# The mask as the start value of each dot, and a divided unit's first part added by TensorE (graph attention on one Trainium2 core)

## The chip, the core and the metric

The kernel runs on one core of a Trainium2 chip. Five engines run at the same time, each with its own in-order queue: TensorE (PE, with a separate row PEld for its weight loads), VectorE (DVE), ScalarE (ACT), GpSimd (POOL) and SyncE (SP, which here only issues transfers). They wait for each other by semaphores. The metric is the device time of one execution, in microseconds (us). Before the change the median of 12 runs is 2206.37 us (2199.12 to 2210.2).

## What is computed

Two graph attention layers over 2048 nodes with 256 channels and 8 batches. A node attends only to its neighbours in `adj`, each layer adds its input and normalises. The change touches layer 0 only:

```python
h1 = x @ W1; h2 = x @ W2; h3 = x @ W3
e = einsum('bnd,bmd->bnm', h1, h2)
e = leaky_relu(e, 0.2)
e = where(adj > 0, e, -1e12)
h_prime = softmax(e) @ h3
x = layernorm(x + relu(h_prime))
```

Layer 1 has four heads and additive scores (a term of the row plus a term of the neighbour), then softmax, weighted sum, elu and a layer norm.

## The kernel before

A node has on average about 17 neighbours, so nothing dense is computed. In the set-up, nodes are counted and sorted by their number of neighbours and cut into 16 tiles of 128 nodes, one node to a partition. Tile t gets `SLOTS[t]` neighbour slots (36 down to 11); slot k of a tile is a gather of 128 rows, the k-th neighbour of each node. Where a node has fewer neighbours than its tile has slots, `neg` (128 partitions by 291 columns, one column to a slot, made at L553) holds -3.0e38 instead of 0, and the slot's index points nowhere, so that the row keeps what stood there.

The work unit is a tile and one half of the batches (4 of 8). Layer 0 runs 16 units of the first half (h = 0), then 16 of the second; layer 1 runs its 32 units behind them. Within a layer 0 unit:

- `own_rows` and `before0` fetch the tile's own rows, turn them (PE, evicted by ACT) and project them with W1 W2^T to `u.g` (PE L437, evicted by ACT at L642).
- GpSimd issues one gather per slot (L200) into a ring of buffers; a buffer comes free when PE has used it in the sum.
- `logits0` takes the slots in order. `dots` (L648) forms, for each slot and each of 4 batches, the product of the gathered row and `u.g` summed over 256 channels: one DVE instruction (L651), followed by a read of its accumulator into one column of the score tile `e`. When all slots of a part are there, leaky relu (L692), mask (L693), maximum (L702) and subtraction (L703) follow on DVE, and ACT makes the exponential.
- `weights0` sums and divides. `weighted` makes of each weight a diagonal of 64 columns on ACT (L861, four per slot).
- `sums0` multiplies diagonals and gathered rows on PE and adds them up in two PSUM accumulators per part (`add_slot`, L825).
- `after0`: `whole` brings the sum to `u.hs`, `turn_h` turns it on PE, `project_h` multiplies with W3 (PE L437), `residual` adds the input and takes statistics (DVE L979, L982), then the norm (ACT L415) and the query projection for layer 1 (PE L1020).

A unit with `SLOTS` of 16 or more (11 of the 16 tiles; t = 0 too, which has 26 main slots and one slot for all of its further neighbours) is divided: `parts` has two entries, each with its own softmax so that the first part's sum can start early. When the second part's maximum and sum are known, the first part's share is known too. At the fifth slot of the second part ACT writes the first part's accumulators, scaled by that share, to `u.hs` (L948):

```python
if i == 1 and k == 4:
    u.hs = hs_rows
    ...
        u.hs[:, ts(2 * r + j, C)], u.accs[0][r][:, ts(j, C)], AF.Copy,
```

and after the last slot DVE adds the second part's accumulators (L962, two additions of 128x512). For a unit that is not divided ACT copies the accumulators (L966).

The order on DVE, ACT and PE is written by the kernel itself: `tick` advances a clock by one per slot of `sums0`, and in each tick it takes what is due. `due(distance, stage)` puts a stage that many ticks ahead: `whole` 4 ticks after a divided unit's last slot, `turn_h` 2 ticks later, `project_h` 4 more. The dots of later units are interleaved in this order. In each queue an instruction that waits holds up all behind it. The tile t = 0 has a path of its own for its further neighbours: `extra_logits0` forms their dots at L651 as well (8 of them, against `u.gx` in PSUM), and `into_place` (L748) copies the spread result into `e`.

The 2248 dots against `u.g` are 281 main slots by 4 batches by 2 halves.

Of the kernel before, what the change touches and what calls it, by code (L numbers as in the profile page):

```python
# [19 lines left out]
ALU = mybir.AluOpType  # L20
# [4 lines left out]
P = 128  # L25
# [15 lines left out]
EXTRA = SLOTS[0] - MAIN  # L41
# [95 lines left out]
def fast_path(  # L137
# [24 lines left out]
    nc = tc.nc  # L162
    B, N, C = x.shape
    NT = N // P
    KC = C // P
    HB = B // 2
    HC = HB * C
    MOST = 2 + MAIN // 2 + EXTRA
    HG = HB * H
    HW = HC // 2  # L170
    CD = C + H
    QW = 2 * CD
    offs = [sum(SLOTS[:t]) for t in range(NT)]
# [53 lines left out]
    held = [ring_tile(f"held_{i}") for i in range(MORE)]  # L227
# [3 lines left out]
    ident = w.ident  # L231

    g_rows = held[0][:, : 2 * HC].rearrange("p (i c) -> p i c", i=2)
    xo_rows, hs_rows = held[1][:, :HC], held[1][:, HC : 2 * HC]

    twice = const.tile([P, 64], F32, tag="twice", name="twice")
    nc.vector.tensor_tensor(twice, ident[:, :64], ident[:, 64:], ALU.add)
# [3 lines left out]
    for it in range(NT):  # L241
        r = ring_tile(f"adj_{it}")
# [56 lines left out]
    for it in range(NT):  # L299
# [6 lines left out]
        i = it // 2  # L306
# [31 lines left out]
    neg = const.tile([P, total], F32, tag="neg", name="neg")  # L338
# [4 lines left out]
    for r in range(2):  # L343
        rr = slice(64 * r, 64 * r + 64)
        pr = ps_tile(f"ps_half_{r}")[:, :NT]
        for c in range(2):
            nc.tensor.matmul(
                pr[64 * c : 64 * c + 64],
                lhsT=ident[rr, rr],
                rhs=ranked[rr, 0, :],  # L350
                start=True,
                stop=True,
                tile_position=(64 * r, 64 * c),
# [66 lines left out]
    def due(distance, stage, *args):  # L420
        heappush(events, (clock[0] + distance, len(stamps), partial(stage, *args)))
        stamps.append(None)
# [222 lines left out]
            yield  # L645
        u.ready = True

    def dots(u, rows, others, into):  # L648
        for b in range(HB):
            jt = sp.tile([P, C], BF16, tag="j", name=f"j_{u.name}_{clock[0]}_{b}", bufs=4)  # L650
            nc.vector.tensor_tensor_reduce(  # L651
                out=jt,
                in0=rows[:, ts(b, C)],
                in1=others(b),
                scale=1.0,
                scalar=0.0,
                op0=ALU.mult,
                op1=ALU.add,
                accum_out=into(b),
            )  # L660

    def logits0(u):

        while not u.ready:
            yield 0
        for i, part in enumerate(u.parts):
            n, o = f"{u.name}_{i}", offs[u.t] + part.at
            K = part.wide
            if i == 0:
                both = ep.tile([P, 2, HB, MOST], F32, tag="e", name=f"e_{n}")  # L670
            e = both[:, i, :, : 1 + K + 1]
            if part.extra:
                yield from extra_logits0(u, i, e)
            for k in range(part.main):
                if i == 0 and k == part.main - 4 and u.parts[-1].extra:
                    due(0, spread_g, u)
                c, s = part.where(k)
                while len(u.chunks[i]) <= c:
                    yield 0
                while clock[0] < u.chunks[i][c][2] + 3:  # L680
                    yield 0
                dots(
                    u,
                    u.chunks[i][c][0][:, s, :],
                    lambda b: u.g[:, ts(b, C)],
                    lambda b, k=k: e[:, b, 1 + k : 2 + k],
                )
                yield 1
            while part.extra and not u.placed:
                yield 0  # L690
            p = e[:, :, 1 : 1 + K]
            nc.vector.scalar_tensor_tensor(p, p, ALPHA, p, ALU.mult, ALU.max)  # L692
            nc.vector.tensor_tensor(  # L693
                p, p, neg[:, o : o + K].unsqueeze(1).to_broadcast([P, HB, K]), ALU.add
            )
            v = p
            if i:
                v = e[:, :, : 1 + K]
                nc.vector.tensor_copy(e[:, :, 0], u.m[0])
            m = sp.tile([P, HG], F32, tag="m1", name=f"m_{n}")[:, :HB]  # L700
            u.m.append(m)
            nc.vector.tensor_reduce(m, v, AX.X, ALU.max)  # L702
            nc.vector.tensor_tensor(  # L703
                v, v, m.unsqueeze(2).to_broadcast([P, HB, v.shape[2]]), ALU.subtract
            )
            due(2, nc.scalar.activation, v, v, AF.Exp)
            due(4, weights0, u, i, K, e, m)
            yield 0
# [9 lines left out]
    def extra_logits0(u, i, e):  # L718
        main = u.parts[i].main
        while not u.chunks[i] or u.gx is None:  # L720
            yield 0
        while clock[0] < u.chunks[i][0][2] + 3:
            yield 0
        b = wide_tile(f"xe_{u.name}")
        x, ex = b[:, :HB], b[:, 16 : 16 + HB * EXTRA]
        ex = ex.rearrange("p (b k) -> p b k", b=HB)
        dots(
            u,
            u.chunks[i][0][0][:, 0, :],
            lambda b: u.gx[b // 2][:, ts(b % 2, C)],  # L730
            lambda b: x[:, b : b + 1],
        )
        nc.vector.tensor_tensor(
            ex,
            x.unsqueeze(2).to_broadcast([P, HB, EXTRA]),
            place.unsqueeze(1).to_broadcast([P, HB, EXTRA]),
            ALU.mult,
        )

        def to_rows():  # L740
            pe = ps_tile(f"ps_xe_{u.name}")[:, : HB * EXTRA]
            nc.tensor.matmul(
                pe, lhsT=of_one, rhs=b[:, 16 : 16 + HB * EXTRA], start=True, stop=True
            )
            due(2, into_place, pe)

        def into_place(pe):
            nc.vector.tensor_copy(  # L748
                e[:, :, 1 + main : 1 + main + EXTRA], pe.rearrange("p (b k) -> p b k", b=HB)
            )  # L750
            u.placed = True

        due(1, to_rows)
        yield 1
# [76 lines left out]
                        tile_position=(64 * r, 64 * c),  # L831
                    )

    def add_extra(acc, rows, lhsT, width):
        for r in range(2):
            for j in range(2 * C // width):
                for c in range(2):
                    rhs = rows[:, ts(2 * c + j, C)]
                    if width > C:
                        rhs = rows[:, ts(c, 2 * CD)].rearrange("p (j w) -> p j w", j=2)[:, :, :C]  # L840
                    nc.tensor.matmul(
                        acc[r][64 * c : 64 * c + 64, ts(j, width)],
                        lhsT=lhsT(r, c, j),
                        rhs=rhs,
                        start=False,
                        stop=(j == 2 * C // width - 1),
                        tile_position=(0, 64 * c),
                    )

# [74 lines left out]
    def sums0(u):  # L924
        u.accs = []
        for i, part in enumerate(u.parts):
            acc = None
            for k in range(part.K):
                while len(u.diags) <= part.at + k:
                    yield 0  # L930
                if acc is None:
                    acc = [acc_tile(f"acc_{u.name}_{i}_{r}") for r in range(2)]
                diag = u.diags[part.at + k]
                c, s = part.where(k) if k < part.main else (0, 0)
                rows, n, _ = u.chunks[i][c]
                if k < part.main:
                    add_slot(acc, k, part.K, rows[:, s, :], diag)
                else:
                    add_extra(
                        acc, rows[:, 0, :], lambda r, c, j: diag[r][:, 2 * c + j, :], C  # L940
                    )
                if s == n - 1:
                    credits[0] += 1
                if i == 1 and k == 4:
                    u.hs = hs_rows
                    for r in range(2):
                        for j in range(2):
                            nc.scalar.activation(  # L948
                                u.hs[:, ts(2 * r + j, C)], u.accs[0][r][:, ts(j, C)], AF.Copy,
                                scale=u.fs[:, r, j : j + 1],  # L950
                            )
                yield 1
            u.accs.append(acc)

    def after0(u):
        h, t, n = u.h, u.t, u.name

        def whole():
            if len(u.parts) == 2:
                for r in range(2):  # L960
                    v = u.hs[:, ts(r, HW)]
                    nc.vector.tensor_tensor(v, v, u.accs[1][r], ALU.add)  # L962
            else:
                u.hs = hs_rows
                for r in range(2):
                    nc.scalar.copy(u.hs[:, ts(r, HW)], u.accs[0][r])  # L966
# [86 lines left out]

        split = len(u.parts) == 2
        at = 4 if split else 2
        due(at, whole)
        due(at + 2, turn_h)
        due(at + 6, project_h)
# [320 lines left out]
    for j, u in enumerate(units):  # L1379
# [9 lines left out]
        if 2 <= j < 10:  # L1389
            b, i = divmod(j - 2, 2)  # L1390
# [317 lines left out]
```

## Time and profile before

| | us |
|---|---|
| median of 12 runs | 2206.37 |
| the profiled execution, its own time | 2207.72 |
| its span, first to last instruction | 2206.0 |
| set-up, 0 to 118: DVE busy | 73.08 |
| layer 0, 118 to 1255: DVE / PE / ACT / POOL busy | 1051.49 / 1018.50 / 817.71 / 715.56 of 1137 |
| layer 1, 1255 to 2206: DVE / PE / ACT / POOL busy | 832.49 / 658.16 / 526.61 / 702.16 of 951 |
| dots L651: busy, and their accumulator reads | 798.0 and 180.0 |
| mask additions L693, 54 of them: busy | 11.1 |
| additions L962, 44 of them: busy | 28.1 |
| diagonals L861, 2248 of them on ACT: busy | 570.3 |

The granted TensorE clock is 0.912 of full speed over the span. "Busy" is the time covered by an engine's records; records of consecutive DVE instructions overlap by some tens of nanoseconds, since the next starts before the last has drained, so sums of record lengths come out above the time that they hold the engine. A group line gives line, engine, operation, what it writes from what, shapes, count, then busy us, mean ns of one, and the idle time of the engine just before with what ended it.

### The profile page before, as it was taken

The numbers are of one execution on the slowest core, as the hardware profiler recorded it, in microseconds if no ns is written. First come the engines' busy times: TensorE is split into PE (matmuls) and PEld (weight loads), VectorE is DVE, ScalarE is ACT, GpSimd is POOL, SyncE is SP. The second block draws the span as 40 slices with busy tenths as digits, with TensorE's granted clock in tenths as the row PEclk, the third lists the DMA queues.
The fourth block names the chain that finished last, engine by engine and source line by source line (L and its number), as shares of the span: only waits on it lengthen the run. The fifth ranks groups of instructions, "written<-read, shape, count | busy, mean of one in ns | idle before, by whom it ended". The sixth has DMA issues, their size and how long they took to land. (4 is left out here: it accounts for less than half of the span.)

```text
span 2206.0 us, 50366 instructions
## 1 busy us (share of the span) xinstructions
PE 1696.7 (77%) x16096; PEld 917.2 (42%) x16096; DVE 1957.1 (89%) x6803; ACT 1399.1 (63%) x4801; POOL 1459.9 (66%) x1423
## 2 busy tenths in 40 slices
PE   0328798989889999999999887766666667776764
PEld 0215566656656666767666532221221212222221
DVE  7578889999999987799999779997987988998996
ACT  6306587768667776888888676543565656554545
POOL 3355476666666665667667577777777777777773
PEclk9659999999999999999999999898888898888887
DMA  9987899999998898999999899999999999999991
GB/s 389 316 276 247 307 336 386 351 333 332 330 320 291 305 326 272 347 347 361 341 350 343 289 380 367 344 345 353 388 359 346 363 371 363 379 348 356 367 339 58
DMA packets 240192, 734.76 MB, mean 333 GB/s; under 512 B 53984, under 2 KB 63328, under 8 KB 237488
## 3 DMA queue, kind: packets, MB, share of 16 engines
q0 software_dynamic: 183296, 645.85, 79.9%
q1 hardware_dynamic: 55360, 84.44, 11.5%
q8 instruction: 131, 2.15, 0.4%
q10 hardware_dynamic: 1264, 1.18, 0.2%
q14 instruction: 141, 1.16, 0.1%
HBM read 674.53 MB, written 76.09 MB: 340 GB/s over the span
## 5 line engine op out<-in xcount | busy, mean ns | idle before, releaser
L200 POOL DMA_INDIRECT s<-xg,idx x564 | 597.2, 1059 | 369.4 <-PE acc L825 134.2
L651 DVE CUSTOM_DVE_ANT_0 j<-s,held 128x256 bf16<-128x256 f32 x2248 | 798.0, 419 | 44.3 <-DMA s<-xg,idx 33.4
L825 PE MATMUL acc<-s,ident 64*64 64x512 f32 x4496 | 610.8, 685 | 262.8 <-DVE s L908 160.1
L200 POOL DMA_INDIRECT s<-qg,idx x564 | 574.4, 1018 | 181.4 <-issue 123.1
L825 PE MATMUL acc<-s,dg 64*64 64x256 f32 x8992 | 598.1, 394 | 69.1 <-ACT dg L861 68.6
L861 ACT ACTIVATE dg<-twice,e 128x64 f32<-128x64 f32 x2248 | 570.3, 341 | 36.8 <-PE acc L825 18.7
L908 DVE TENSOR_TENSOR s<-s,p 128x2048 f32<-128x2048 f32 (+1 forms) x246 | 542.4, 2208 | 0.1
L825 PEld LDWEIGHTS acc<-s,ident 64*64 64x64 f32 x4496 | 182.2, 151 | 679.7 <-issue 353.0
L825 PEld LDWEIGHTS acc<-s,dg 64*64 64x64 f32 x8992 | 342.0, 136 | 282.6 <-ACT dg L861 137.2
L898 ACT ACTIVATE s<-s,e 128x64 f32<-128x64 f32 x1376 | 342.5, 335 | 69.8 <-DVE e L1163 56.3
L1359 ACT ACTIVATE e<-e 128x40 f32<-128x40 f32 (+19 forms) x88 | 27.6, 313 | 285.1 <-DVE e L1143 185.3
L651 DVE DVE_READ_ACCUMULATOR2_ANT e<- 128x1 f32 x2248 | 180.0, 80 | 0.0
L208 POOL DMA_INDIRECT out_dram<-o,oidx x128 | 126.8, 991 | 64.2 <-ACT o L415 28.6
L1020 PE MATMUL ps_q<-wqs,x1T 128*128 128x264 f32 x512 | 136.7, 411 | 18.2 <-DVE y L979 11.3
L437 PE MATMUL ps_p_g<-held,xT 128*128 128x256 f32 x512 | 122.6, 394 | 0.0
L437 PE MATMUL ps_p_h<-held,hT 128*128 128x256 f32 x512 | 119.5, 386 | 0.0
L1087 DVE TENSOR_TENSOR e<-s,own 128x32 f32<-128x32 f32 (+1 forms) x290 | 52.8, 185 | 75.0 <-DMA s<-qg,idx 74.5
L1020 PEld LDWEIGHTS ps_q<-wqs,x1T 128*128 128x128 f32 x512 | 95.2, 196 | 57.4 <-issue 15.9
L1359 ACT COPY held<-ps_q 128x264 f32<-128x264 f32 x128 | 47.3, 379 | 104.1 <-PE ps_q L1020 93.3
L437 PEld LDWEIGHTS ps_p_g<-held,xT 128*128 128x128 f32 x512 | 97.5, 195 | 23.5 <-issue 8.1
L437 PEld LDWEIGHTS ps_p_h<-held,hT 128*128 128x128 f32 x512 | 95.0, 190 | 24.8 <-issue 12.4
L397 ACT ACTIVATE z<-st,roots 128x4 f32<-128x4 f32 x64 | 19.0, 297 | 126.8 <-DVE st L1266 99.1
(190 smaller groups left out, 1550.5 us busy)
## 6 DMA issues: line engine op xcount, KB each, us to landing
adj<-in_adj_dram SPq DMA_DIRECT2D x16, 1024.0 KB
xr<-held SPq DMA_DIRECT2D x128, 128.0 KB
x1s<-y SPq DMA_DIRECT2D x32, 512.0 KB
xr<-x1s SPq DMA_DIRECT2D x32, 512.0 KB
s<-xg,idx POOLq DMA_INDIRECT x564
s<-qg,idx POOLq DMA_INDIRECT x564
edges<-adj SPq DMA_DIRECT2D x16, 512.0 KB
xg<-in_x_dram SPq DMA_DIRECT2D x4, 2048.0 KB
```

Source lines behind the costliest of these rows:

```text
L200: nc.gpsimd.indirect_dma_start(out=dst, out_offset=None, in_=table, in_offset=AT(ap=index, axis=0), bounds_check=table.shape[0] - 1, oob_i ...
L208: ins = nc.gpsimd.indirect_dma_start(out=table, out_offset=AT(ap=index, axis=0), in_=src, in_offset=None)
L397: nc.scalar.activation(z, var, AF.Ln, bias=w.roots[:, 0:1], scale=1.0 / C)
L437: nc.tensor.matmul(pp[:, ts(j, C)], lhsT=srcT[:, ts((2 * i + j) * KC + k, P)], rhs=weight[:, k, :], start=(k == 0), stop=(k == KC - 1),)
L651: nc.vector.tensor_tensor_reduce(out=jt, in0=rows[:, ts(b, C)], in1=others(b), scale=1.0, scalar=0.0, op0=ALU.mult, op1=ALU.add, accum_out ...
L825: nc.tensor.matmul(out, lhsT=lhsT, rhs=rhs, start=(k == 0 and j == 0), stop=(k == K - 1 and (j == 1 or diag is None)), tile_position=(64 * ...
L861: nc.scalar.activation(diag[:, b, :], twice, AF.Copy, scale=u.p[i][:, b, k : k + 1])
L898: nc.scalar.activation(v[:, a, g, :], v[:, a, g, :], AF.Copy, scale=pv[:, a, g : g + 1])
L908: nc.vector.tensor_tensor(v, v, pv.unsqueeze(3).to_broadcast([P, n, H, D]), ALU.mult)
L1020: nc.tensor.matmul(pq[:, : C + 2 * H], lhsT=u.x1T[:, ts(i * KC + k, P)], rhs=w.sqs[:, k, j * H : j * H + CD + H], start=(k == 0), stop=(k ...
L1087: nc.vector.tensor_tensor(e[:, k : k + ns, :].rearrange("p s (b g) -> p s b g", b=HB), rows[:, :ns, :].rearrange("p s (b w) -> p s b w", b ...
L1359: heappop(events)[2]()
```

## The change

Two edits to layer 0, and their small consequences.

First, `dots` takes an argument `first`, the scalar that each sum starts from. In `logits0` it is the slot's column of `neg`, one value per partition; the mask's addition after the leaky relu goes. The masked sums therefore start from -3.0e38 and pass through the leaky relu. For the further neighbours of t = 0, `into_place` adds their columns of `neg` where it copied. Two `memset`s in the set-up clear the unused columns at the end of two held buffers, which later join the ring.

Second, for a divided unit of the first half (`joined`), four matmuls with the identity, put right after the unit's last slot, add `u.hs` into the second part's accumulators, which are left open for it (`last`), and `whole` copies them to `u.hs` on ACT in place of the two additions on DVE.

```diff
+    for r in held[:2]:
+        nc.gpsimd.memset(r[:, 2 * HC :], 0.0)
...
-    def dots(u, rows, others, into):
+    def dots(u, rows, others, into, first=0.0):
...
-                scalar=0.0,
+                scalar=first,
...
                     lambda b, k=k: e[:, b, 1 + k : 2 + k],
+                    neg[:, o + k : o + k + 1],
                 )
...
             nc.vector.scalar_tensor_tensor(p, p, ALPHA, p, ALU.mult, ALU.max)
-            nc.vector.tensor_tensor(
-                p, p, neg[:, o : o + K].unsqueeze(1).to_broadcast([P, HB, K]), ALU.add
-            )
...
         def into_place(pe):
-            nc.vector.tensor_copy(
-                e[:, :, 1 + main : 1 + main + EXTRA], pe.rearrange("p (b k) -> p b k", b=HB)
-            )
+            o = offs[u.t] + u.parts[i].at + main
+            nc.vector.tensor_tensor(
+                e[:, :, 1 + main : 1 + main + EXTRA],
+                pe.rearrange("p (b k) -> p b k", b=HB),
+                neg[:, o : o + EXTRA].unsqueeze(1).to_broadcast([P, HB, EXTRA]),
+                ALU.add,
+            )
...
+    def joined(u):
+        return u.h == 0 and len(u.parts) == 2
...
+                last = not (i == 1 and joined(u))
                 if k < part.main:
-                    add_slot(acc, k, part.K, rows[:, s, :], diag)
+                    add_slot(acc, k, part.K + (not last), rows[:, s, :], diag)
...
+        def join():
+            for r in range(2):
+                for c in range(2):
+                    nc.tensor.matmul(
+                        u.accs[1][r][64 * c : 64 * c + 64, :],
+                        lhsT=ident[:, ts(c, 64)],
+                        rhs=u.hs[:, ts(r, HW)],
+                        start=False,
+                        stop=True,
+                        tile_position=(0, 64 * c),
+                    )
+
         def whole():
-            if len(u.parts) == 2:
+            if joined(u):
+                for r in range(2):
+                    nc.scalar.copy(u.hs[:, ts(r, HW)], u.accs[1][r])
+            elif len(u.parts) == 2:
...
+        if joined(u):
+            due(0, join)
         due(at, whole)
```

More of the change, by code (lines that the diff above doesn't have):

```diff
@@ L832, in add_slot, with add_extra @@
                     )
-    def add_extra(acc, rows, lhsT, width):
+    def joined(u):
+        return u.h == 0 and len(u.parts) == 2
+    def add_extra(acc, rows, lhsT, width, last=True):
         for r in range(2):
@@ L845, in add_extra @@
                         start=False,
-                        stop=(j == 2 * C // width - 1),
+                        stop=(last and j == 2 * C // width - 1),
                         tile_position=(0, 64 * c),
@@ L935, in sums0 @@
                 rows, n, _ = u.chunks[i][c]
+                last = not (i == 1 and joined(u))
                 if k < part.main:
-                    add_slot(acc, k, part.K, rows[:, s, :], diag)
+                    add_slot(acc, k, part.K + (not last), rows[:, s, :], diag)
                 else:
                     add_extra(
-                        acc, rows[:, 0, :], lambda r, c, j: diag[r][:, 2 * c + j, :], C
+                        acc, rows[:, 0, :], lambda r, c, j: diag[r][:, 2 * c + j, :], C, last
                     )
```

## The prediction

> **What bounds the kernel now.** I read the page's busy shares first, then a table by stage, then what VectorE (DVE) waits for in the first layer, then the groups of instructions and their order in time.
>
> ```profile
> PE 1696.7 (77%) x16096; PEld 917.2 (42%) x16096; DVE 1957.1 (89%) x6803; ACT 1399.1 (63%) x4801; POOL 1459.9 (66%) x1423
> ```
> ```profile
> core 0: us, PE busy (x) PEld busy (x) DVE busy (x) ACT busy (x) POOL busy (x), PEclk, DMA share, GB/s
> 118.00:700.00 582.00, 488.69 (x5118) 328.82 (x5120) 540.34 (x2836) 378.77 (x1352) 356.29 (x338) 0.92 0.91 320
> 700.00:1255.00 555.00, 529.80 (x5973) 362.66 (x5969) 511.15 (x2717) 438.95 (x1577) 359.27 (x339) 0.99 0.95 330
> ```
>
> DVE is the busiest engine overall. The dots run from 119.5 to 1250.6 us; I call 118 to 1255 layer 0, and about 700 is where its second half of batches begins. DVE is busy 540.3 of 582 us and 511.2 of 555 us there: 1051.5 of 1137, which leaves 85.5 us idle. TensorE (PE) is nearly as full in the second half (529.8 of 555), but its records are modelled, so I ask who waits for whom. These are DVE's own waits from 118 to 1255 (us in total, times, longest), then two waits of the other engines on it in the same stretch:
>
> ```profile
> DVE j L651 <- DMA s<-xg,idx: 33.4, 30, 7.5
> DVE y L979 <- PE ps_p_h L437: 18.4, 7, 10.6
> DVE j L651 <- ACT held L642: 10.7, 6, 5.3
> DVE s L763 <- ACT e L1359: 5.8, 5, 2.1
> ```
> ```profile
> ACT e L1359 <- DVE e L703: 86.8, 19, 22.2
> PE acc L825 <- ACT dg L861: 66.3, 44, 22.7
> ```
>
> ACT waits 86.8 us for the last DVE step of a softmax (L703), and PE waits 66.3 us for the diagonals that ACT makes from it: a chain that starts in DVE. DVE's own waits are short and few. So in layer 0 a DVE microsecond is mostly a kernel microsecond. What DVE does there (count, busy us and mean ns):
>
> ```profile
> L651 DVE CUSTOM_DVE_ANT_0 j<-s,held 128x256 bf16<-128x256 f32 x2248 | 798.0, 419 | 44.3 <-DMA s<-xg,idx 33.4 <-ACT held L642 10.7
> L301 DVE TENSOR_SCALAR_CACHE_REDUCE junk<-keys,key 128x2048 f32<-128x2048 f32 x8 | 18.7, 2340 | 5.0 <-issue 5.0
> L367 DVE TENSOR_SCALAR_CACHE_REDUCE listless<-neg 128x291 f32<-128x291 f32 x1 | 0.4, 441 | 0.0
> L598 DVE SCALAR_TENSOR_TENSOR ones<-extras 128x128 f32<-128x128 f32 x1 | 0.4, 352 | 0.0
> L692 DVE SCALAR_TENSOR_TENSOR e<-e 128x92 f32<-128x92 f32 x2 | 0.5, 248 | 0.0
> ```
>
> The dots are 2248 instructions of one form. Records overlap, so I cost by start to start, from the timeline (start us, length us):
>
> ```profile
> 145.96 0.42 DVE L651 CUSTOM_DVE_ANT_0 j<-s,held 128x256 bf16<-128x256 f32 x1
> 146.30 0.08 DVE L651 DVE_READ_ACCUMULATOR2_ANT e<- 128x1 f32 x1
> 146.42 0.20 DVE L692 SCALAR_TENSOR_TENSOR e<-e 128x44 f32<-128x44 f32 x1
> 146.66 0.20 DVE L693 TENSOR_TENSOR e<-e,neg 128x44 f32<-128x44 f32 x1
> 146.89 0.20 DVE L702 TENSOR_REDUCE m<-e 128x4 f32<-128x44 f32 x1
> ```
> ```profile
> 62.22 2.34 DVE L301 TENSOR_SCALAR_CACHE_REDUCE junk<-keys,key 128x2048 f32<-128x2048 f32 x1
> 64.49 0.08 DVE L301 DVE_READ_ACCUMULATOR junk<-keys,key 128x1 f32 x1
> ```
>
> A dot holds DVE 0.345 us (145.96 to 146.30, and the same in every run of dots). An element costs 1.04 ns: the in-place products of L908 take 2277 ns for 2048 and 1212 for 1024. So 256 elements are 266 ns, and 79 ns are fixed.
>
> **The change, part by part.** *A per-partition scalar in every dot.* The 2248 dots of L651 get `neg[:, k]`, a column read from memory, where the constant 0.0 stood. Their number and the accumulator reads stay. No dot of before has such a scalar, but other DVE instructions have. L301 compares with a column of `key`: start to accumulator read is 64.49 - 62.22 = 2.27 us, less 2048 x 1.04 = 2.13, leaves 140 ns fixed, 61 more than the dot's 79. L367 is the same operation with constants: 441 - 291 x 1.04 = 138 ns beyond its elements by record, against 2340 - 2130 = 210 for L301: 72 more. L598 has a column (352 ns for 128 elements), L692 of the same operation has constants: 248 + 36 x 1.04 = 285, so 67 more. Three pairs say 61 to 72 ns. That none of them is the dot's own operation is the doubt; the lower bound is 0 (the read is hidden under the accumulator read in front of it), the upper 80. I take 61, the one pair measured start to start: 2248 x 0.061 = +137 us on DVE, half of it in each half.
>
> *The mask's addition goes.* 54 instructions L693, in a chain where each waits for the last: 146.66 to 146.89, 0.23 to 0.28 us each, say 0.24: -13 us on DVE. For the two extra slots the copy L748 (193 ns) becomes an addition (L693 takes 202 at that size): nothing.
>
> *TensorE adds the first part.* 11 units of the first half are divided (SLOTS of 16 and more). In each, two L962 additions leave DVE. One pair held it from 358.96 to 360.16 us, 1.20: 11 x 1.20 = -13 us. PE gets four matmuls of 128 rows, 64 columns and 512 wide per unit. The nearest rows are L841's of that shape: 592 ns each, eight within 1.94 us where two column groups run side by side. So 1.0 to 2.4 us per unit, 11 to 26 us in all. ACT gets two copies of 128x512 per unit at L966's 580 ns: 22 x 0.58 = 13 us. I cost both at nothing: from 118 to 700 us PE is idle 582 - 488.7 = 93 us and ACT 203 us, and the slower dots add to that. The matmuls stand right behind the unit's last slot, and their operand was written by ACT at the fifth slot of the second part, so they wait for nothing new; behind them on PE stand the projections of a later unit. The copies come four ticks later, when the diagonals already made for the next unit have forced PE past them; behind them on ACT stand the next diagonals. Were that cover gone, it would be up to +26 on PE or +13 on ACT.
>
> *Two memsets* on GpSimd (32 columns, 128 columns take 0.19 us) fall before a stretch at 3.65 to 8.33 us in which it waits: nothing.
>
> One rule stands against these rows. The Trainium skill ("VectorE: DVE Perf Modes", section "Rules for kernel authors") says of chained DVE operations: "Minimize op *count*, not sems". By count alone the change takes 54 + 22 = 76 operations off DVE and would give -26 us; the rows of L301 and L598 say that one kind of operand can outweigh the count.
>
> *The sum.* DVE: +137 - 13 - 13 = +111 us. Not all of it reaches the end, since a slower DVE finds data ready that it waited for. Without the first dot's 7.5 us, 26 us of waits on gathers, 18 on PE's projections and 16 on ACT's evictions and exponentials can shrink: 60 us. The waits at the start (24 us on gathers before 300) and the one of 10.6 us on PE are of the kind that shrink; I take off 35. That leaves +76 us on layer 0. Layer 1 changes in nothing but its start. The profiled execution took 2207.7 us (span 2206.0), 1.3 above the median of the runs shown, so 2207.7 + 76 is 2284 by it; I say 2283.
>
> **The rivals.** *The column is free in a dot.* A dot is a custom operation with an accumulator read in front; the scalar could be fetched there. Then only the removals are left: -26 on DVE, perhaps 5 of it lost to waits: 2186 us, faster. For it: no dot of before shows the price. Against it: L301 is also followed by an accumulator read, stands behind an independent small cast that it overlaps, and still shows 61 ns. It decides below 26 / 2248 = 12 ns per dot; from there on the change is slower. Chance 0.14.
>
> *It is paid in part, or slack takes most of it.* PE at 529.8 of 555 us and DMA at shares of 0.91 and 0.95 say that layer 0 is close to three bounds. If all 60 us of DVE's waits vanish, or the price is 25 to 40 ns: 111 - 60 = +51, or 2248 x 0.03 - 26 = +41, with less absorbed: +20 to +50, 2228 to 2258. Against it: ACT and PE wait for DVE longer than it for them. Chance 0.12.
>
> *The join stalls.* If PE's matmuls or ACT's copies held up the diagonals and g's evictions, +26 and +13 would come on top: 2207.7 + 76 + 39 = 2323. For it: ACT already delays dots by 10.7 us. Against it: the idle time above. Chance 0.06. That the change does not do what it says is not a rival: the instruction lists of the two programs differ in these instructions alone.
>
> **How the numbers follow.** The forecast (the column is paid in full, 55 to 80 ns) has 0.68; its own range is 2258 to 2335: 55 ns with 60 us absorbed is 124 - 26 - 60 = +38, 80 ns with 20 absorbed is 180 - 26 - 20 = +134, and the ends of both together are unlikely. To hold 8 in 10 the range takes in most of the partial case, 2238 to 2335. What is left out is the free column and the tails. A measurement here can tell about 0.2% (4.4 us) from no change. Faster 0.14, within 0.2% 0.02, slower 0.84.
>
> **What would show it.** The dots' mean goes from 419 to about 480 ns, their start to start from 0.345 to about 0.405. The waits on gathers and on PE's projections shrink, ACT's wait for L703 and PE's for diagonals grow, DVE's busy share of layer 0 rises above 95%, and the end of the dots moves from 1251 to about 1327 us; the stretch behind it keeps its 951 us. Dots that still start every 0.345 us would make the whole forecast wrong; dots at 0.405 with layer 0 less than 40 us longer would make the absorption wrong.

## The result, and the profile after

The changed kernel takes 2292.67 us (median of 8 runs, 2289.04 to 2295.33) against 2206.23 us for the kernel before in the same comparison: a ratio of 1.0391, with a 95% interval of 1.0381 to 1.0401. That is 86 us slower, where 76 were forecast. The profiled execution took 2292.5 us with a span of 2290.7 us.

Two groups of the profile after, in the form of those shown before: the dots, now with `neg` among their inputs, and their accumulator reads.

```profile
L653 DVE CUSTOM_DVE_ANT_0 j<-s,held,neg 128x256 bf16<-128x256 f32 x2248 | 935.3, 479 | 19.9 <-DMA s<-xg,idx 8.8 <-ACT xT L1384 7.7 <-ACT held L644 3.2
...
L653 DVE DVE_READ_ACCUMULATOR2_ANT e<- 128x1 f32 x2248 | 176.8, 79 | 0.0
```

The same 2248 dots have a mean of 479 ns where they had 419, and 935.3 us busy where they had 798.0. DVE's timeline after (start us, length us) shows what one costs:

```profile
500.07 0.48 DVE L653 CUSTOM_DVE_ANT_0 j<-s,held,neg 128x256 bf16<-128x256 f32 x1
500.48 0.08 DVE L653 DVE_READ_ACCUMULATOR2_ANT e<- 128x1 f32 x1
500.48 0.48 DVE L653 CUSTOM_DVE_ANT_0 j<-s,held,neg 128x256 bf16<-128x256 f32 x1
500.89 0.08 DVE L653 DVE_READ_ACCUMULATOR2_ANT e<- 128x1 f32 x1
...
501.70 0.48 DVE L653 CUSTOM_DVE_ANT_0 j<-s,held,neg 128x256 bf16<-128x256 f32 x1
502.11 0.08 DVE L653 DVE_READ_ACCUMULATOR2_ANT e<- 128x1 f32 x1
```

From 500.07 to 502.11 are five dots, so 0.408 us each against 0.345 before (0.407 over longer runs of them). That is 62 ns more for each dot, 2248 x 0.062 = 139 us. The table by stage, with the same columns as before (busy us and count of PE, PEld, DVE, ACT, POOL, then clock, DMA share, GB/s), cut where the second half and layer 1 begin now:

```profile
118.00:742.00 624.00, 508.86 (x5184) 335.88 (x5182) 591.02 (x2797) 387.76 (x1369) 353.69 (x338) 0.91 0.86 299
742.00:1345.00 603.00, 551.27 (x6039) 373.60 (x6041) 575.61 (x2686) 447.10 (x1598) 363.44 (x343) 0.96 0.90 306
```

DVE is busy 1166.6 of 1227 us, 95.1% (92.5% before). Its idle time in layer 0 fell from 85.5 to 60.4 us, so 25 us of the extra work went into gaps. DVE's waits from 118 to 1345 us, and those of the others on it:

```profile
DVE y L1002 <- PE ps_p_h L439: 18.3, 4, 9.6
DVE j L653 <- DMA s<-xg,idx: 8.8, 11, 1.5
DVE j L653 <- ACT xT L1384: 7.7, 1, 7.7
...
DVE j L653 <- ACT held L644: 3.2, 4, 1.2
```
```profile
ACT e L1384 <- DVE e L703: 105.7, 23, 23.4
...
PE acc L829 <- ACT dg L868: 87.5, 43, 25.7
```

The wait on gathers fell from 33.4 to 8.8 us, the one on g's evictions from 10.7 to 3.2; the one on PE's projections stayed at 18.3. ACT's wait on DVE grew from 86.8 to 105.7 and PE's on the diagonals from 66.3 to 87.5. The last dot starts at 1336.5 us against 1250.6, 85.9 later (1327 was forecast), and from there to the end of the span it is 954.2 us against 955.4. So all of the loss lies in front of that last dot, in layer 0.

### The profile page after: what moved, and what is told of

It is laid out like the page before. It is cut to its first block, busy times and chain, and to the rows that moved or that the text cites. A ratio compares the mean times of both kernels' runs of the same rounds, so it can differ in the third digit from the quotient of the medians.

```text
span 2290.7 us, 50473 instructions
## 1 busy us (share of the span) xinstructions
PE 1734.1 (76%) x16184; PEld 932.8 (41%) x16184; DVE 2070.3 (90%) x6727; ACT 1411.7 (62%) x4823; POOL 1458.4 (64%) x1425
## 5 line engine op out<-in xcount | busy, mean ns | idle before, releaser
L653 DVE CUSTOM_DVE_ANT_0 j<-s,held,neg 128x256 bf16<-128x256 f32 x2248 | 935.3, 479 | 19.9 <-DMA s<-xg,idx 8.8
L829 PE MATMUL acc<-s,dg 64*64 64x256 f32 x8992 | 610.9, 401 | 89.6 <-ACT dg L868 88.6
L829 PEld LDWEIGHTS acc<-s,dg 64*64 64x64 f32 x8992 | 349.1, 139 | 311.0 <-ACT dg L868 160.6
```

Of the source, the lines that this page charges most:

```text
L653: nc.vector.tensor_tensor_reduce(out=jt, in0=rows[:, ts(b, C)], in1=others(b), scale=1.0, scalar=first, op0=ALU.mult, op1=ALU.add, accum_o ...
L829: nc.tensor.matmul(out, lhsT=lhsT, rhs=rhs, start=(k == 0 and j == 0), stop=(k == K - 1 and (j == 1 or diag is None)), tile_position=(64 * ...
```

## The experiments

Each result is a median beside the kernel before in the same comparison, and the ratio to it with its 95% interval. The kernels of one comparison ran on one chip; kernels of different comparisons are set against each other by their ratios.

### e1, the mask alone

```diff
     def joined(u):
-        return u.h == 0 and len(u.parts) == 2
+        return False
```

> The changed kernel with no unit joined: the mask is still the start value of every dot, and DVE adds the first part as before (22 additions back). Theory (the column costs 62 ns in each of 2248 dots, +139 us on DVE, -13 for the mask's addition, some 27 us of DVE's waits absorb part; the join is worth its 13 us of DVE): 13 us longer than the changed kernel, 2300 to 2306 us, dots every 0.407 us. Rival (the join gives back on PE or ACT what it saves on DVE): the same as the changed kernel, 2293 us, or less.

2299.76 us against 2205.6, ratio 1.0432 (1.0416 to 1.0448). The mask's part accounts for all of the loss and more. Against the changed kernel, the join takes 7 us off by the medians, 9 by the ratios (1.0432 to 1.0391), where its 22 additions are 13 us on DVE: the theory is right in kind, but a third to a half of the gain is given back. The rival, that all of it is given back, is out.

### e2 and e11, the join alone

The kernel before with the hunks for `joined`, `last`, `join` and `whole` and the two memsets only; e11 is the same kernel a second time.

```diff
-                    neg[:, o + k : o + k + 1],
...
+            nc.vector.tensor_tensor(
+                p, p, neg[:, o : o + K].unsqueeze(1).to_broadcast([P, HB, K]), ALU.add
+            )
```

(The diff is against the changed kernel; `into_place` copies again.)

> The kernel before with the join alone (constant 0.0 in the dots, mask added behind). Theory: 13 us off DVE, of which waits take up to half: 2193 to 2200 us, ratio 0.994 to 0.997. Rival (PE and ACT stall on 44 matmuls and 22 copies, up to 26 and 13 us): 2206 to 2230 us. Second rival (the first half has slack enough to hide it): 2206 us.

> The kernel of e2 (join in the first half alone) a second time, as the candidate that beats both kernels: 2196 to 2204 us, ratio 0.997 to 0.999. If the gain of 5 us was chance, 2204 to 2208 us.

2198.99 us against 2205.6, ratio 0.9977 (0.9966 to 0.9988); the second time 2202.41 against 2204.07, ratio 0.9990 (0.9981 to 0.9999). Both intervals lie below 1, so it beats both kernels, by 2 to 5 us of the 13 that it takes off DVE; the expected 0.994 to 0.997 was too much. The second half's first dot starts at 713.4 us in e2 and 712.7 in e11, against 720.9 before, 7 to 8 us earlier and not 13. Where DVE has its constant in the dots, it is not DVE alone that sets the end of the first half.

### e3, a column of zeros

```diff
+    zero = const.tile([P, 1], F32, tag="zero", name="zero")
+    nc.gpsimd.memset(zero, 0.0)
...
-    def dots(u, rows, others, into):
+    def dots(u, rows, others, into, first=0.0):
...
-                scalar=0.0,
+                scalar=first,
...
                     lambda b, k=k: e[:, b, 1 + k : 2 + k],
+                    zero,
```

> The kernel before with nothing changed but that the dots' start value is read from a column of zeros in place of the constant 0.0 (the same numbers come out; the two memsets are there too). Theory (the read of a column costs 62 ns whatever stands in it and wherever it comes from): dots every 0.407 us, +139 us on DVE, less some 27 us of absorbed waits: 2310 to 2325 us. Rival (the price comes with the columns of neg, which DVE itself wrote earlier, or with the values -3.0e38): dots near 0.345 us and 2206 us.

2311.97 us against 2205.6, ratio 1.0483 (1.0467 to 1.0499). The dots of this kernel, in the groups of its profile:

```profile
L655 DVE CUSTOM_DVE_ANT_0 j<-s,held,zero 128x256 bf16<-128x256 f32 x2248 | 935.7, 481 | 19.2 <-DMA s<-xg,idx 16.5 <-ACT held L646 2.3
```

A mean of 481 ns, though the numbers are those of the kernel before and the column is one that GpSimd wrote once. So the form of the operand costs the time, not `neg`, its values or who wrote it. The rival is out. All these dots have 256 elements, so no run tells a price per instruction from a price per element; the prediction's three pairs, 61 to 72 ns at 128 to 2048 elements, speak for a price per instruction, in other operations. The same run gives the worth of the mask's addition when the column is paid anyway: from e3 to e1 the ratio falls by 0.0051, 11 us of the 13 that the additions hold DVE.

### e4, the constant back

```diff
-                    neg[:, o + k : o + k + 1],
```

> The changed kernel with the constant 0.0 back in the dots and no mask at all for the main slots (the masking of layer 0's main slots is left out; its addition stays away too). Theory (the column alone makes the change slower): dots every 0.345 us, DVE 26 us lighter than before, 2180 to 2195 us. Rival (something else in the change costs, the join or the later first part): above 2206 us.

2194.08 us against 2205.6, ratio 0.9950 (0.9937 to 0.9964). In its profile the dots are back at their old length:

```profile
L653 DVE CUSTOM_DVE_ANT_0 j<-s,held 128x256 bf16<-128x256 f32 x2248 | 797.5, 420 | 46.9 <-DMA s<-xg,idx 35.7 <-ACT held L644 10.9
```

So the column alone makes the change slower: with a constant in its place the rest of the change is 11 us faster than the kernel before. That is at the upper edge of what was expected, and less than half of the 26 us taken off DVE. Against e2 it lacks 54 mask additions and is 0.0027 faster, 6 us of 13. Since e4 leaves the mask of layer 0's main slots out altogether, these 6 us are about what a mask that costs DVE nothing could bring here.

### e5, two columns

```diff
-                scale=1.0,
-                scalar=0.0,
+                scale=1.0 if first is not zero else one,
+                scalar=first,
```

> The kernel with a column of zeros as the dots' start value, and the dots' factor (constant 1.0) read from a column of ones as well: two columns in each dot. Theory A (each column is fetched by itself before the elements flow): dots every 0.47 us, another +139 us on DVE, some 2440 us. Theory B (the 62 ns are one trip for all columns of an instruction): dots every 0.407 us or a little more, the same time as with one column, some 2315 us.

2436.71 us against 2204.56, ratio 1.1057 (1.1040 to 1.1074). Its timeline on DVE:

```profile
500.73 0.54 DVE L655 CUSTOM_DVE_ANT_0 j<-s,held,zero 128x256 bf16<-128x256 f32 x1
501.20 0.08 DVE L655 DVE_READ_ACCUMULATOR2_ANT e<- 128x1 f32 x1
501.20 0.54 DVE L655 CUSTOM_DVE_ANT_0 j<-s,held,zero 128x256 bf16<-128x256 f32 x1
501.66 0.08 DVE L655 DVE_READ_ACCUMULATOR2_ANT e<- 128x1 f32 x1
```

500.73, 501.20 and 501.66: 0.465 us from dot to dot, and a mean of 540 ns in the groups. The second column costs 58 to 60 ns on top of the first one's 62, so each is paid by itself, as theory A has it; what the engine does in that time, no run shows. It is also a dose: about 132 us more on DVE made the kernel 127 us longer (1.1057 - 1.0483 = 0.0574 of 2205), nearly one for one, where the first column's 139 us made it 106.

### e7, the column in the first half only

On the kernel of e3:

```diff
-                    zero,
+                    zero if u.h == 0 else 0.0,
```

> The column of zeros in the dots of the first half only (1124 of 2248). Theory (each half absorbs its share): half of what the column costs in both halves, +50 to +58 us, 2256 to 2264 us. Rival (the slack lies at the start, where DVE waits 24 us for gathers, so the first half absorbs nearly all): +40 to +45 us, 2246 to 2251 us.

2262.46 us against 2204.56, ratio 1.0267 (1.0251 to 1.0283). Both forms of dots stand side by side in its groups:

```profile
L655 DVE CUSTOM_DVE_ANT_0 j<-s,held,zero 128x256 bf16<-128x256 f32 x1124 | 469.3, 481 | 19.5 <-DMA s<-xg,idx 18.2 <-ACT held L646 1.3
L655 DVE CUSTOM_DVE_ANT_0 j<-s,held 128x256 bf16<-128x256 f32 x1124 | 397.1, 420 | 12.5 <-ACT held L646 8.4 <-DMA s<-xg,idx 3.9
```

481 ns with the column, 420 without, in one execution. Each half's dots cost DVE 1124 x 0.062 = 70 us more. By the times, the first half passes 58 or 59 of them on, the second (e3 less e7, 0.0216 of 2205) 48. The traces put the two closer together: the second half's first dot starts at 720.9 us before, 774.5 in e7 and 775.4 in e3, and the last dot at 1250.6, 1304.0 and 1355.5, so that in e3 the first half grows by 54 us and the second by 50. The rival, by which the waits at the start let the first half absorb nearly all of what is absorbed (+40 to +45 us), is out. Which half absorbs more is not settled: in e9, whose first half is that of the kernel before, the second half begins 2.3 us earlier, so a few microseconds of one trace say little.

### e6, e10, e8 and e9: the join in the second half

e6, and e10 once more beside e9 and e11: the join of e2, in both halves.

```diff
-        return u.h == 0 and len(u.parts) == 2
+        return len(u.parts) == 2
```

> The kernel before with the join in both halves of layer 0 (22 units, 44 additions fewer on DVE, 88 matmuls and 44 copies more). Theory (DVE bounds both halves): twice the gain of the join in the first half alone, 2180 to 2195 us. Rival (PE is nearly full in the second half, 529.8 of 555 us, and the matmuls cost it 1 to 2.4 us per unit): no more than the gain of the first half, or up to 26 us worse than that.

> The kernel of e6 beside e9 and e11: 2217 to 2226 us again. Less than e11 by no amount under either theory; if PE is the cause, e10 lies above e11 by about what e9 lies above the kernel before, less the 13 us that DVE saves.

e8, and e9 once more: the join of e2, in the second half alone, with DVE copying the sum out.

```diff
-        return u.h == 0 and len(u.parts) == 2
+        return u.h == 1 and len(u.parts) == 2
...
-                    nc.scalar.copy(u.hs[:, ts(r, HW)], u.accs[1][r])
+                    nc.vector.tensor_copy(u.hs[:, ts(r, HW)], u.accs[1][r])
```

> The kernel before with the join in the second half alone, and DVE, not ACT, copying the joined sum out (two copies of 128x512 per unit in place of its two additions, about as long): PE gets 11 x 1.87 us = 20.6 us more in the second half, DVE and ACT keep theirs. Theory (PE bounds the second half, and its matmuls are what made the join in both halves 22 us slower than in the first alone): +18 to +28 us, 2223 to 2233 us. Rival (ACT's 22 copies, 13 us and their place in its queue, are what cost it): +0 to +6 us, 2205 to 2211 us.

> The same kernel as e8 once more, beside the two it is to be compared with: on the chip of e8 the kernel before itself took 2478 us, so that run does not say what bounds the second half at 2205 us. The join in the second half alone, DVE copying the joined sum out: PE +20.6 us there, DVE and ACT unchanged. Theory (PE bounds the second half): +18 to +28 us, 2223 to 2233 us. Rival (ACT's copies are what costs): +0 to +6 us, 2205 to 2211 us.

| kernel | us | kernel before | ratio (95%) |
|---|---|---|---|
| e6, both halves | 2221.09 | 2204.56 | 1.0076 (1.0062 to 1.0089) |
| e10, the same again | 2219.63 | 2204.07 | 1.0062 (1.0048 to 1.0076) |
| e8, second half, DVE copies | 2481.2 | 2477.7 | 1.0012 (0.9997 to 1.0027) |
| e9, the same again | 2215.57 | 2204.07 | 1.0060 (1.0046 to 1.0074) |

On the chip of e8 the kernel before itself took 2478 us, and the join's cost there is not clear of noise, so e8 is set aside; e9, e10 and e11 share a chip. What a join costs PE stands in the timeline of the changed kernel, around its first join:

```profile
365.57 1.94 PE L969 MATMUL acc<-held,ident 128*64 128x512 f32 x8
367.44 0.92 PE L439 MATMUL ps_p_g<-held,xT 128*128 128x256 f32 x3
```

Four matmuls leave eight records and hold PE 1.87 us, 20.6 us for 11 units. In the second half PE has little room for it. DVE's waits there, first in e9 (700 to 1255 us), then in e10 (700 to 1268 us), where the kernel before had 13.2 us on `ps_p_h` and 5.5 on ACT's exponentials:

```profile
DVE y L1000 <- PE ps_p_h L439: 19.4, 8, 10.6
...
DVE s L765 <- ACT e L1382: 5.5, 4, 2.1
```
```profile
DVE y L1000 <- PE ps_p_h L439: 28.0, 10, 10.6
DVE s L765 <- ACT e L1382: 9.3, 6, 2.1
```

In e10 PE is busy 549.2 of the 568 us of that stretch and DVE only 493.7. With DVE's load left as it was (e9), PE's 20.6 us make the kernel 11 to 13 us slower. Moving the copies to ACT as well takes 13 us off DVE and brings nothing: by the ratios it is 16 us from e11 to e10 and 22 from e2 to e6, of which the first is not clear of e9's 13. The traces are clearer. From the first to the last dot of the second half it is 529.7 us before, 528.3 in e2 and 529.0 in e11 (which leave this half alone), 538.0 in e9, and 544.7 and 544.8 in e10 and e6. So PE's matmuls with DVE's load unchanged are 8 us, and the copies on ACT 7 more, although DVE has 13 us less to do.

For e6 the theory (2180 to 2195 us) is out, and its rival, up to 26 us worse than the join in the first half alone, came true. For e9 neither side met its number (18 to 28, or 0 to 6 us). For e10 the theory let it lie above e11 by e9's 13 us less the 13 that DVE saves, so by nothing, and it lies 16 above. PE's matmuls are therefore shown to cost the second half time; that ACT's copies and their wait on PE are the rest is not shown by a run of their own.

## Why the prediction was right, point by point

**The column in every dot: right.** The forecast took 61 ns from L301, which is another operation; the dot's own price is 62 ns. That the pairs by record (67 and 72) said a little more made no difference. The doubt, that no row of before showed the dot itself with a column, is settled by e3, and the rival of the free column falls with it: its 2186 us is near e4's 2194, the kernel in which the column really is absent. That another operation gave the price to 1 ns is in part luck: the three pairs spread over 11 ns, 25 us of the sum.

**The mask's addition goes: right in size, conditional in worth.** -13 us on DVE; with the column in the dots it was worth 11 (e3 to e1), with constants 6 (e2 to e4).

**TensorE adds the first part: costed at nothing on PE and ACT, and this step was too kind.** The join was worth 7 to 9 us in place of 13 (e1 to the changed kernel), 2 to 5 without the column. The bounds on PE were also misread: the eight records within 1.94 us at L841 were taken for eight matmuls, and are four, so that the low end of 1.0 us per unit did not exist; 1.87 was measured. The rival that the join stalls, up to 39 us, did not come about, since the join still gains; the error stayed small because only the first half was joined. In the second half the cover named for it (idle time on PE) is nearly missing, and e6 and e10 show what it costs then.

**What does not reach the end: 35 us forecast, 27 measured.** On DVE the whole change is 139 - 13 - 13 = +113 us; the kernel became 86 us longer. Taken as one, the term was 8 us too large, and with the 2 us of the column that is the distance from 2283 to 2293. Taken apart, it was nearer: the column alone lost 33 of its 139 us on the way (e3), and the two removals brought 18 to 20 us in place of 26, a loss that the forecast did not have. But 35 was a choice among 60 us of waits, not worked out, so that it came this close is luck too. Which waits would shrink was half right: the gathers' did (33.4 to 8.8), g's evictions' did, the one on PE's projections did not move (18.4 to 18.3), and a wait of 7.7 us on a turned input was new.

**The rival of three close bounds.** It priced slack at up to 60 us, which was too much, but its reason, that PE is nearly full in the second half, was borne out for the join (e9). For the column it mattered less: the first half, where PE had 93 us idle, and the second each passed on most of their 70 us.

**The rule on counts.** The Trainium skill ("VectorE: DVE Perf Modes", "Rules for kernel authors") has "Minimize op *count*, not sems". In e4, where DVE sees 76 operations fewer and hardly any other change, the kernel is 11 us faster, so the rule holds as far as it goes; one operand's form in 2248 instructions outweighed it about ten times (106 us in e3).

## What to carry to other kernels

Before a scalar is turned from a constant into a per-partition column, count the instructions: here the column cost 62 ns each, with `neg` and with zeros alike, so folding one short operation into many instructions pays only while the folded operation is longer than 62 ns times their number (about 0.24 us against 42 x 0.062 = 2.6 us for each part here). Look for the price in another operation of the same engine that already has such an operand, and compare from start to start, not by record lengths, which overlap. What a microsecond on the busiest engine is worth is not fixed: on DVE it was about 0.5 (e2 to e4), 0.76 (e3, 106 of 139) and 0.95 (e5) of a microsecond of the kernel, rising as DVE was loaded.

## What was not expected of the hardware

Two columns in one instruction are paid one by one: a dot takes 0.345, 0.407 and 0.465 us with none, one and two. A matmul of 128 rows, 64 columns and 512 values in float32 leaves two records of 592 ns each, and four of them on two column groups hold PE 1.87 us. And the kernel before took 2478 us on one chip against 2204 to 2206 on the others. The same program was traced on both, as e8 and e9: the dots have means of 419 and 418 ns, and the second layer's 64x512 matmuls 681 ns in both, but these matmuls cover 820.6 us in e8 and 607.8 in e9, so fewer of them ran at the same time. The cause stays open.
